# Attention scores in groups of up to three halves, five buffers of exps, single buffers for three other tiles

## The chip, the cores and the metric

The kernel runs on one core of a Trainium2 chip. The metric is the device time of one execution in microseconds. TensorE (PE) does the matmuls, VectorE (DVE), ScalarE (ACT) and GpSimd (POOL) the elementwise work, and SyncE (SP) issues the DMAs of the main part.

## The reference

One adaptive-LayerNorm transformer block in float32, for two batches of 2048 tokens with width 256. Attention has 16 heads with keys of 16 and values of 64; the softmax runs over the *queries* (axis 1 of `bnhm`), so its sum belongs to a key and can be folded into that key's row of values. The feed-forward part quantizes its inputs and weights to FP4 in blocks of 16 and has a hidden width of 704.

```python
mod = (silu(c) @ wmod).reshape(2, 6, 1, 256)
sa, ca, ga, sb, cb, gb = mod[:, 0], ..., mod[:, 5]
# ga and gb are kept at least 0.25 away from zero, with their signs
h = layernorm(x) * (1 + ca) + sa
q, k, v = h @ query_proj, h @ key_proj, h @ value_proj     # 16 heads: 16, 16, 64
sim = einsum('bnkh,bmhk->bnhm', q, k)                      # n query, m key
attn = softmax(sim / 4, axis=1)                            # over the queries
x = x + ga * (einsum('bnhm,bmhv->bnhv', attn, v) @ output_proj)
h = layernorm(x) * (1 + cb) + sb
gate, y = fp4(h) @ fp4(w_gate).T, fp4(h) @ fp4(w_up).T
x = x + gb * (fp4(silu(gate) * y) @ fp4(w_down).T)
```

## The kernel before

**The steps.** Attention is cut into 512 steps: 2 batches x 16 heads x 16 tiles of 128 keys. A step computes 128 x 2048 scores (keys on partitions, queries along the row), in two *halves* of 1024 queries. `scores` (L1009) issues the four matmuls of a step to PSUM: a half is two matmuls of 512 queries, which run as two row tiles of 64 rows (the keys and queries are stacked in a high and a low part). `step` (L1036) then
- evacuates each half with one DVE instruction, which scales, copies it to the exp buffer `e` in SBUF and keeps the minimum of each row,
- joins the two minima on POOL (`mn`),
- takes the exp of all 2048 in place on ACT, with the sum `z`,
- takes the reciprocal `rz` on DVE and scales the key's 64 values by it on POOL (`vn`),
- multiplies on PE: `o` accumulates 64 x 2048 over the 16 steps of a head, as products of `vn` with `e`, in two parts `j` of two column tiles of 64 columns.

So PE has three tilings: two row tiles for scores ("rows"), two column tiles for o, values, projections and most of the other products ("columns"), and the full array, for transposes among others.

**Other work.** Beside the steps run: LayerNorm and q, k projections (`norm`, `qk`, L903, whose results go through `st` to a scratch in DRAM), the values of each group of four heads (`load_wv`, L968, and `values`, L976), the projection of a group of four heads back to x (`load_wo`, L1117, and `project`, L1126), the exact quantization of the weights (beside the first batch's steps), and the feed-forward part of batch 0 (`ffn`, L1240), beside the steps of batch 1. After the last step come the last projection and the feed-forward part of batch 1 (`tail`, L1354).

**What sets the order.** All instructions of PE, DVE, ACT and POOL are emitted by a planner, `Order` (L102), when the program is built. Each piece of work is a generator that yields its next operation or a `Wait` for keys and for *rooms*, which are counted buffers. `rooms` (L367) has 3 places `s` in PSUM for halves of scores, 2 for `o`, 4 for `e`, 2 for heads and so on. The planner keeps a clock for every engine with estimated costs (`estimate`, L269). In `run` (L166) it looks at all chains that can go on, takes for each engine the one with the earliest *due time* among those that could start within a small patience, and emits the operation of the engine that starts first. The engines then work through their queues in that order, with semaphores where data or buffers need them. A room holds the time at which it comes free by the estimates.

The due time of `scores` and `step` is the step's number i; the products with the values get `due(i + LAG)` (L1073), with `LAG = 4.0`. `scores` takes two places and emits the two halves of a step as one list (L223 emits a list without a break), so no other matmul comes between them. A room of `e` is taken by `step` before the first evacuation and given back after the second part of o.

All operations are made by one helper, so that the profile shows line 255 for nearly all of them; tiles' names tell them apart: `ps` scores, `e` exps, `o` products, `vn` scaled values, `v` values, `op` projections, `st` the q, k store.

Of the kernel before, what the change touches and what calls it, by code (L numbers as in the profile page):

```python
# [10 lines left out]
F32 = mybir.dt.float32  # L11
F32R = mybir.dt.float32r
# [8 lines left out]
P = 128  # L21
# [5 lines left out]
CHANGE = 0.1  # L27
PDVE = 0.04
PACT = 0.05
LAG = 4.0  # L30
HALF = 0.22
WPACE = 0.5
NPACE = 0.2
# [28 lines left out]
class Op:  # L62
    def __init__(self, engine, cost, emit, delay=0.0, table=None, mode=None, port=False):
        self.engine, self.cost, self.emit = engine, cost, emit
        self.delay, self.table, self.mode = delay, table, mode
        self.port = port


class Either:
# [32 lines left out]
class Order:  # L102
# [17 lines left out]
    def add(self, gen, due, pace=0.0):  # L120

        heapq.heappush(self.later, (due, next(self.seq), gen, pace))


    def signal(self, key, of=1, early=0.0):

        n, t = self.counts.get(key, (0, 0.0))
        n, t = n + 1, max(t, self.chain.end - early)
        self.counts[key] = (n, t)
        if n == of:  # L130
            self.done[key] = t
        return n == of

    def give(self, name, n=1, place=0):
        for _ in range(n):
            heapq.heappush(self.rooms[name], (self.chain.end, place))

    def due(self, due):
        self.chain.due = due
# [26 lines left out]
    def run(self):  # L166
        while self.later or self.active:
            while self.later and self.later[0][0] <= self.step + self.ahead:
                due, _, gen, pace = heapq.heappop(self.later)
                c = Chain(gen, due, pace)  # L170
                self.active.append(c)
                self.advance(c)
            best, times = {}, {}
            for c in sorted(self.active, key=lambda c: c.due):
                if not self.settle(c):
                    continue
                what = c.what
                free = isinstance(what, Free)
                what = what.op if free else what
                found = []  # L180
                for op in what.ops if isinstance(what, Either) else (what,):
                    ops = op if isinstance(op, list) else [op]
                    e = ops[0].engine
                    start = max(self.clock[e], c.base)
                    if not free and c.engine is not None:
                        start = max(start, c.end + (self.SAME[e] if e == c.engine else self.CROSS))
                    if e == "PE":
                        times[id(ops)] = start
                        if ops[0].mode != self.mode:
                            t = max(start, self.clock[e] + self.DRAIN[self.mode])  # L190
                            times[id(ops)] = t + self.LOAD[ops[0].mode]
                            start = max(start, self.clock[e] + CHANGE)
                    if ops[0].port:
                        start = max(start, self.port)
                    found.append((start, c.due, next(self.seq), c, ops))
                if isinstance(what, Best):
                    ends = [f[0] + sum(op.cost for op in f[4]) for f in found]
                    first = ends[0] - what.margin
                    found = [found[0] if first <= min(ends[1:]) else found[1]]
                for f in found:  # L200
                    best.setdefault(f[4][0].engine, []).append(f)
            if not best:
                if not self.later:
                    raise RuntimeError(
                        "no chain can go on: "
                        + str([(c.due, vars(c.what)) for c in self.active[:20]])
                    )
                self.step = self.later[0][0] - self.ahead
                continue
            picks = []  # L210
            for e, found in best.items():
                first = min(f[0] for f in found)
                start, due, _, c, ops = min(
                    (f for f in found if f[0] <= first + self.patience.get(e, 0.0)),
                    key=lambda f: f[1:3],
                )
                picks.append((start, due, next(self.seq), c, ops))
            start, _, _, c, ops = min(picks)
            e = ops[0].engine
            t = start  # L220
            if e == "PE":
                t = times[id(ops)]
            for op in ops:  # L223
                if op.table is not None and op.table != self.table:
                    t, self.table = t + self.TABLE, op.table
                op.emit()
                t += op.cost
            self.clock[e] = t
            if ops[-1].port:
                self.port = t  # L230
            if e == "PE":
                self.mode = ops[-1].mode
            c.end, c.engine = t + ops[-1].delay, e
            c.due += c.pace
            self.advance(c, e)
# [81 lines left out]
def adaln_block(  # L317
# [41 lines left out]
        for n, e in (  # L359
# [6 lines left out]
    )  # L366
    order = Order(  # L367
        rooms=dict(
            misc=MISC, s=3, o=2, e=4, head=2, osb=1, v=5, x=2, wv=2, wo=2,
            h=2, qm=2, h2=2, h2t=1, hqt=1, st=2, qs=3, ln=2,  # L370
        ),
        ahead=AHEAD,
        patience={"PE": PPE, "DVE": PDVE, "ACT": PACT},
# [7 lines left out]
    ps_s = ctx.enter_context(tc.tile_pool(name="ps_s", bufs=1, space=PSUM))  # L381
    hp = ctx.enter_context(tc.tile_pool(name="hp", bufs=1))
    headp = ctx.enter_context(tc.tile_pool(name="headp", bufs=2))
    spool = ctx.enter_context(tc.tile_pool(name="spool", bufs=4))
    op_ = ctx.enter_context(tc.tile_pool(name="op", bufs=3))
    vp = ctx.enter_context(tc.tile_pool(name="vp", bufs=5))
    w2 = ctx.enter_context(tc.tile_pool(name="w2", bufs=2))
# [2 lines left out]
    def banks(place, name):  # L390

        return ps_s.tile([P, 2, 512], F32, tag=f"s{place}", name=name)
# [13 lines left out]
    def matmuls(dst, pairs, first=True):  # L406
        return [
            T.matmul(dst, lhsT=l, rhs=r, start=(first and k == 0), stop=(k == len(pairs) - 1))
            for k, (l, r) in enumerate(pairs)
        ]  # L410
# [492 lines left out]
    def qk(b, blk, i, n):  # L903
# [20 lines left out]
        if room == "v":  # L924
            st = vp.tile([P, 4, QV], F32, tag="v", name=name).bitcast(F32R)
            st = st.rearrange("p (r u) n -> p r (u n)", r=2)
        else:
            st = w2.tile([P, 2, 512], F32R, tag="st", name=name)
        yield A.copy(st[:, 0, :], ps)
        yield V.tensor_tensor(st[:, 1, :], ps, st[:, 0, :], ALU.subtract)  # L930
        leave(place)
# [35 lines left out]

    def load_wv(b, q):  # L968
        yield Wait(take=["wv"])
        wvs[b, q] = op_.tile([P, KC, QV], F32, tag="wv", name=f"wv{b}_{q}", bufs=2)  # L970
        yield S.dma_start(
            wvs[b, q], wv[:, q * QV : (q + 1) * QV].rearrange("(k p) n -> p k n", p=P)
        )
        signal(("wv", b, q))
# [31 lines left out]

    halves = {}

    def scores(i, b, h, m):  # L1009

        if (b, h) == (0, 0):
            yield Wait(["first q", ("first k", m // 4)])
        else:
            yield Wait([("head", b, h)])
        if i > 0:
            yield Wait([("s", i - 1, 1)])
        order.step = i
        q, k = heads[b, h]
        places = yield Wait(take=["s", "s"], early=HALF)
        ops = []  # L1020
        for u, place in enumerate(places):
            ps = banks(place, f"ps{b}_{h}_{m}_{u}")
            halves[i, u] = ps, place
            for g in range(2):
                rows = slice(64 * g, 64 * (g + 1))
                ops += matmuls(
                    ps[:, g, :],
                    [(k[rows, m * P : (m + 1) * P], q[rows, u * 512 : (u + 1) * 512])],
                )
        yield Free(ops)  # L1030
        for u in range(2):
            signal(("s", i, u), early=0.0 if u else HALF)
        if m == NT - 1:
            give("head")

    def step(i, b, h, m):  # L1036

# [78 lines left out]

    def load_wo(b, q):  # L1117
        yield Wait(["mods"], ["wo"])
        w = wos[b, q] = op_.tile([P, 2, D], F32, tag="wo", name=f"wo{b}_{q}", bufs=2)
        yield S.dma_start(w, wo[q * QV : (q + 1) * QV, :].rearrange("(k p) n -> p k n", p=P))  # L1120
        for j in range(2):
            yield Free(G.tensor_tensor(w[:, j, :], w[:, j, :], mod(b, "ga"), ALU.mult)) if j else \
                G.tensor_tensor(w[:, j, :], w[:, j, :], mod(b, "ga"), ALU.mult)
        signal(("wo", b, q))
# [343 lines left out]
        add(values(0, 0, g), -5 if g == 0 else 4 * g - 3)  # L1468
    steps = [(b, h, m) for b in range(B) for h in range(H) for m in range(NT)]
    for i, (b, h, m) in enumerate(steps):  # L1470
        add(scores(i, b, h, m), i)
        add(step(i, b, h, m), i)
        if m == NT - 1:
            add(take_out(b, h), i - 4)
        if m == 2 and i + NT < len(steps):
            add(load_head(*steps[i + NT - m][0:2]), i)
# [101 lines left out]
```

## Time and profile before

| what | value |
|---|---|
| time, median of 3 runs | 1977.5 us (1976.44 to 2165.38) |
| the profiled execution's own time | 1977.45 us |
| its span, first to last instruction | 1975.7 us |
| granted TensorE clock | 0.997 |
| PE busy | 1920.0 us, 97% |
| DVE busy | 1711.3 us, 87% |
| ACT busy | 1325.7 us, 67% |
| POOL busy | 621.0 us, 31% |

A group of the profile reads: line, engine, operation, output<-inputs by tile name, shapes, xcount, then busy time, the mean duration of one in ns, and the idle time of the engine just before these instructions with what ended most of it. PEld are weight loads, which overlap the matmuls. A float32 matmul is two instructions in the profile, and one of scores is one. In a table of stretches, each row has the stretch, its length, and the busy time of PE, PEld, DVE, ACT and POOL with instruction counts, then the clock and the DMA share. In a timeline, each row has start and busy time, with like instructions that follow each other merged.

### The profile page before, as it was taken

To read this page: it belongs to the slowest core of one execution; us is meant where nothing else is said; L and a number is where in the kernel's file an instruction comes from. 1 tells how busy PE (TensorE), PEld (TensorE's weight loads), DVE (VectorE), ACT (ScalarE), POOL (GpSimd) and SP (SyncE) were. 2 spreads that over 40 slices of the span, in tenths; PEclk is the share of its full clock that TensorE was granted. 3 is DMA by queue.
4 is the path that set the end of the run, shared out by engine and by line. 5 is a ranking of instruction groups with operands and counts; after the bars stand their busy time and mean duration, and the time that the engine had idled before them with its cause. 6 is when DMAs were issued, how large, how long until landed. Compare 5 with 4: busy or idle time off the path is not lost. (4 is left out here: it accounts for less than half of the span.)

```text
span 1975.7 us, 30282 instructions
## 1 busy us (share of the span) xinstructions
PE 1920.0 (97%) x10212; PEld 783.1 (40%) x10212; DVE 1711.3 (87%) x4118; ACT 1325.7 (67%) x1419; POOL 621.0 (31%) x1387
## 2 busy tenths in 40 slices
PE   8999999999999989999999999999999999999998
PEld 5323333233333333334333433434443343335666
DVE  5899889989999998778888688898788878997997
ACT  3577766776777676776777667677576867785333
POOL 0233333333344331112445435454343211230010
PEclk9999999999999999999999999999999999999999
DMA  6322121112111122310111201210111111100000
GB/s 213 81 56 58 47 60 49 38 33 49 33 45 33 38 54 75 102 38 25 36 48 46 65 25 46 54 36 16 26 35 43 33 33 33 33 1 1 11 14 19
DMA packets 40394, 88.01 MB, mean 45 GB/s; under 512 B 6320, under 2 KB 22576, under 8 KB 36272
## 3 DMA queue, kind: packets, MB, share of 16 engines
q1 hardware_dynamic: 38880, 83.98, 16.4%
q10 hardware_dynamic: 1360, 2.10, 0.3%
q8 instruction: 82, 1.34, 0.3%
q14 instruction: 72, 0.59, 0.1%
HBM read 63.51 MB, written 20.97 MB: 43 GB/s over the span
## 5 line engine op out<-in xcount | busy, mean ns | idle before, releaser
L255 DVE TENSOR_SCALAR_CACHE_REDUCE e<-ps 128x1024 f32<-128x1024 f32 x1024 | 1221.9, 1218 | 142.1 <-PE ps L255 93.2
L255 ACT ACTIVATE e<-e,mn 128x2048 f32<-128x2048 f32 x512 | 1025.3, 2003 | 436.6 <-POOL mn L255 433.3
L255 PE MATMUL o<-e,vn 128*64 128x512 f32 x4096 | 996.7, 604 | 24.1 <-POOL vn L255 18.5
L255 PEld LDWEIGHTS o<-e,vn 128*64 128x64 f32 x4096 | 253.7, 136 | 482.7 <-issue 351.7
L255 POOL TENSOR_SCALAR mn<-mn 128x1 f32<-128x1 f32 x512 | 154.2, 301 | 834.1 <-DVE rz L255 344.4
L255 PE MATMUL ps<-q,k 64*128 64x512 f32 x2048 | 383.8, 449 | 5.4 <-DVE e L255 2.0
L255 PEld LDWEIGHTS ps<-q,k 64*128 64x128 f32 x2048 | 157.5, 185 | 377.8 <-DVE rz L255 109.5
L255 POOL TENSOR_SCALAR vn<-v,rz 128x64 f32<-128x64 f32 x512 | 169.4, 331 | 307.1 <-DVE rz L255 235.7
L255 PE MATMUL op<-wo,osb 128*64 128x256 f32 (+1 forms) x960 | 125.3, 382 | 2.5 <-DVE x L255 1.8
L255 PE MATMUL v<-wv,ht 128*64 128x256 f32 x1024 | 124.2, 385 | 0.6 <-DVE st L255 0.6
L255 DVE RECIPROCAL rz<-z 128x1 f32<-128x1 f32 x512 | 80.4, 157 | 27.0 <-ACT e L255 25.8
L255 PEld LDWEIGHTS op<-wo,osb 128*64 128x64 f32 (+1 forms) x960 | 76.2, 140 | 60.7 <-issue 30.7
L255 ACT ACTIVATION_READ_ACCUMULATOR e<-e,mn 128x1 f32 x512 | 95.4, 186 | 0.0
L255 PEld LDWEIGHTS v<-wv,ht 128*64 128x64 f32 x1024 | 70.9, 138 | 59.0 <-issue 26.8
L255 DVE DVE_READ_ACCUMULATOR e<-ps 128x1 f32 x1024 | 84.9, 83 | 0.0
L255 ACT COPY osb<-o 64x512 f32<-64x512 f32 x101 | 58.4, 579 | 18.6 <-PE o L255 17.2
L255 PE MATMUL qk<-ht,wqk_sb 128*64 128x512 f32 (+1 forms) x224 | 65.8, 605 | 1.3 <-ACT ht L255 0.9
L255 POOL TENSOR_TENSOR h<-h,m 128x704 f32<-128x704 f32 x32 | 54.1, 1691 | 10.7 <-DVE m L255 6.1
L255 DVE TENSOR_TENSOR x<-op,x 128x1024 f32<-128x1024 f32 (+2 forms) x33 | 37.0, 1122 | 17.8 <-PE op L255 17.6
L255 PE MATMUL dn<-wdb,e 117*128 117x256 f32 (+1 forms) x192 | 45.1, 383 | 3.7 <-ACT e L255 3.7
L255 ACT ACT_TABLE_LOAD x34 | 43.6, 1283 | 4.5 <-issue 3.9
L255 PE MATMUL dn<-wd_t,h2t 117*64 117x256 f32 (+1 forms) x384 | 46.2, 383 | 0.2 <-DVE h2t L255 0.2
(243 smaller groups left out, 1452.4 us busy)
## 6 DMA issues: line engine op xcount, KB each, us to landing
k<-scr SPq DMA_DIRECT2D x124, 256.0 KB, 4.7
scr<-st SPq DMA_DIRECT2D x32, 512.0 KB, 3.1
q<-scr SPq DMA_DIRECT2D x124, 128.0 KB, 5.6
x<-in_x_dram SPq DMA_DIRECT2D x8, 512.0 KB, 4.5
wv<-in_wv_dram SPq DMA_DIRECT2D x8, 256.0 KB, 5.3
wo<-in_wo_dram SPq DMA_DIRECT2D x8, 256.0 KB, 4.1
xt<-in_x_dram SPq DMA_DIRECT2D x4, 512.0 KB, 5.9
out_dram<-h2t SPq DMA_DIRECT2D x16, 128.0 KB, 1.7
```

What stands on the lines that cost most here:

```text
L255: op = Op(self.name, *self.estimate(method, args, kw, lambda: f(*args, **kw)))
```

## The change

`scores` is now one generator for a head instead of one for a step. It takes two places (or one, where only one half is left), as before, and makes a `Group` of the halves. Before the planner emits a group, it asks it to grow: a third half is added if less than three are in it, if a place `s` is free, if that place's time is no later than the estimated time at which the third half would start, and, where the half is the first of a step, if an exp buffer is free by then too. The next group begins where this one ended, so after a group of three the groups straddle two steps, until another group of three or the end of the head.

Beside this, there are five exp buffers instead of four, LAG is 4.5 instead of 4.0, and the tiles `wv` (value weights), `wo` (projection weights) and `st` (q, k store) have one buffer instead of two.

```diff
-LAG = 4.0
+GROUP = 3
+LAG = 4.5
...
+class Group(list):
+    grow = staticmethod(lambda t: False)
...
             if e == "PE":
                 t = times[id(ops)]
+            while isinstance(ops, Group) and ops.grow(t):
+                pass
             for op in ops:
...
-            misc=MISC, s=3, o=2, e=4, head=2, osb=1, v=5, x=2, wv=2, wo=2,
-            h=2, qm=2, h2=2, h2t=1, hqt=1, st=2, qs=3, ln=2,
+            misc=MISC, s=3, o=2, e=5, head=2, osb=1, v=5, x=2, wv=1, wo=1,
+            h=2, qm=2, h2=2, h2t=1, hqt=1, st=1, qs=3, ln=2,
...
-    spool = ctx.enter_context(tc.tile_pool(name="spool", bufs=4))
+    spool = ctx.enter_context(tc.tile_pool(name="spool", bufs=5))
...
-            st = w2.tile([P, 2, 512], F32R, tag="st", name=name)
+            st = w2.tile([P, 2, 512], F32R, tag="st", name=name, bufs=1)
...
-        wvs[b, q] = op_.tile([P, KC, QV], F32, tag="wv", name=f"wv{b}_{q}", bufs=2)
+        wvs[b, q] = op_.tile([P, KC, QV], F32, tag="wv", name=f"wv{b}_{q}", bufs=1)
...
-    def scores(i, b, h, m):
...
+    def scores(i, b, h):
+        n = 0
+        while n < 2 * NT:
+            m = n // 2
...
+            if i + n > 0:
+                yield Wait([("s", i + (n - 1) // 2, (n - 1) % 2)])
+            due(i + n / 2)
+            places = yield Wait(take=["s"] * min(2, 2 * NT - n), early=HALF)
+            group = Group()
...
+            def grow(t):
+                t += sum(op.cost for op in group) - order.CROSS
+                m = n // 2
+                if len(group) == 2 * GROUP or n == 2 * NT or not order.rooms["s"]:
+                    return False
+                if (b, h) == (0, 0) and ("first k", m // 4) not in order.done:
+                    return False
+                if n % 2 == 0 and not (order.rooms["e"] and order.rooms["e"][0][0] <= t):
+                    return False
+                if order.rooms["s"][0][0] > t:
+                    return False
+                half(heapq.heappop(order.rooms["s"])[1])
+                return True
+
+            for place in places:
+                half(place)
+            group.grow = grow
+            first = n - len(places)
+            yield Free(group)
+            order.step = i + (n - 1) // 2
+            for j in range(first, n):
+                signal(("s", i + j // 2, j % 2), early=HALF * (n - 1 - j))
+        give("head")
...
-        w = wos[b, q] = op_.tile([P, 2, D], F32, tag="wo", name=f"wo{b}_{q}", bufs=2)
+        w = wos[b, q] = op_.tile([P, 2, D], F32, tag="wo", name=f"wo{b}_{q}", bufs=1)
...
-        add(scores(i, b, h, m), i)
+        if m == 0:
+            add(scores(i, b, h), i)
```

More of the change, by code (lines that the diff above doesn't have):

```diff
@@ L1007, in adaln_block, with half @@
     halves = {}
-    def scores(i, b, h, m):
[L1011 to L1034, printed above, removed]
+    def scores(i, b, h):
+        n = 0
+        while n < 2 * NT:
+            m = n // 2
+            if (b, h) == (0, 0):
+                yield Wait(["first q", ("first k", m // 4)])
+            elif n == 0:
+                yield Wait([("head", b, h)])
+            if i + n > 0:
[3 more added lines that the diff above has]
+            group = Group()
+            q, k = heads[b, h]
+            def half(place):
+                nonlocal n
+                m, u = n // 2, n % 2
+                n += 1
+                ps = banks(place, f"ps{b}_{h}_{m}_{u}")
+                halves[i + m, u] = ps, place
+                for g in range(2):
+                    rows = slice(64 * g, 64 * (g + 1))
+                    group.extend(
+                        matmuls(
+                            ps[:, g, :],
+                            [(k[rows, m * P : (m + 1) * P], q[rows, u * 512 : (u + 1) * 512])],
+                        )
+                    )
+            def grow(t):
[20 more added lines that the diff above has]
+        give("head")
```

## The prediction

> **What bounds the kernel now.** I read the busy times first, then the costliest groups, then the stretches, then TensorE's own timeline.
>
> ```profile
> PE 1920.0 (97%) x10212; PEld 783.1 (40%) x10212; DVE 1711.3 (87%) x4118; ACT 1325.7 (67%) x1419; POOL 621.0 (31%) x1387
> ...
> L255 DVE TENSOR_SCALAR_CACHE_REDUCE e<-ps 128x1024 f32<-128x1024 f32 x1024 | 1221.9, 1218 | 142.1 <-PE ps L255 93.2
> L255 PE MATMUL o<-e,vn 128*64 128x512 f32 x4096 | 996.7, 604 | 24.1 <-POOL vn L255 18.5
> L255 PE MATMUL ps<-q,k 64*128 64x512 f32 x2048 | 383.8, 449 | 5.4 <-DVE e L255 2.0
> ```
>
> TensorE (PE) is busy 97% of the 1975.7 us span, so it bounds the kernel, with VectorE (DVE) next at 87%. The idle time ahead of the two big groups of matmuls is 24.1 and 5.4 us. Whatever can be won has to be won in PE's own time or in its few waits. The stretches say where those are (columns: length, then busy us of PE, PEld, DVE, ACT, POOL).
>
> ```profile
> 100.00:700.00 600.00, 584.05 (x3076) 208.71 (x3072) 553.58 (x1308) 434.45 (x446) 211.92 (x515) 1.00 0.18 44
> 700.00:1600.00 900.00, 886.27 (x4990) 344.71 (x4990) 755.36 (x1765) 633.17 (x664) 333.80 (x673) 1.00 0.17 44
> 1600.00:1800.00 200.00, 195.21 (x996) 66.71 (x992) 173.56 (x352) 149.61 (x149) 46.15 (x145) 1.00 0.11 25
> ```
>
> From 100 to 1800 us PE is idle for 1700 - 584.05 - 886.27 - 195.21 = 34.5 us. In the first of these stretches DVE is 92% busy (553.58 of 600): there it has little slack. After that it has 16%.
>
> A busy PE isn't a PE at its peak, so I looked at the starts in its timeline (start, then busy us).
>
> ```profile
> 1245.30 0.73 PE L255 MATMUL ps<-q,k 64*128 64x512 f32 x4
> 1245.97 2.80 PE L255 MATMUL o<-e,vn 128*64 128x512 f32 x12
> 1248.69 0.73 PE L255 MATMUL ps<-q,k 64*128 64x512 f32 x4
> 1249.35 2.80 PE L255 MATMUL o<-e,vn 128*64 128x512 f32 x12
> 1252.08 0.73 PE L255 MATMUL ps<-q,k 64*128 64x512 f32 x4
> 1252.74 1.94 PE L255 MATMUL o<-e,vn 128*64 128x512 f32 x8
> ```
>
> PE alternates between two tilings: scores (64*128, two row tiles) and exps times values (128*64, two column tiles). Each visit to the scores is four matmuls, that is two halves. Start to start it takes 0.66 to 0.67 us. Visits of o straight before a visit of scores have medians of 1.009, 1.867 and 2.726 us for 4, 8 and 12 instructions over the whole trace: 0.858 us for each four, and 0.15 us that doesn't grow with the work. That constant part, and its like in the visits to the scores, is what the change is about.
>
> **What the Trainium skill says.** TensorEngine Tiling (Array Packing), section Tiling Modes, says that changing the tiling mode drains TensorE. The trace agrees: those 0.15 us, and the larger sum of 0.24 us worked out below for a visit to the scores. PSUM — Partial Sum Buffer, section Engine vs sequencer instructions, says that the queues of ScalarE, VectorE and GpSimd are strict FIFO, and that matmuls start and complete in program order. The trace agrees as far as it goes: DVE waited 93.2 us for scores, although other work of its own stood behind. So a score whose place isn't free holds all matmuls behind it, and an evacuation without a buffer holds DVE.
>
> **The change part by part.** How often PE changes tiling follows from the two programs' instruction order.
>
> 1. *Third half.* Before, there are 512 visits to the scores, all of two halves. After, 502: 458 of two, 32 of three, 12 of one (an odd last half of a head). Other neighbours shift as well. Changes of tiling, before to after: scores to columns 485 to 483, columns to scores 492 to 473, full array to columns 49 to 39, columns to full 42 to 49, full to scores 20 to 29, scores to full 27 to 19. In all 1115 to 1092.
>    The price of one: single matmuls of a visit to the scores at 606.28 us start at 606.278, 606.617 and (next visit) 606.943. The first matmul is shown as 498 ns and the third as 394, so 0.104 us of the first gap is the entry, and a half alone takes at most 0.337 - 0.104 = 0.233 us. A 512-column matmul of o follows its like after 0.429 us; I take half of its stream for a half of scores, 0.2133 us, an estimate that lies under the bound. So a visit to the scores has 0.663 - 2 x 0.2133 = 0.236 us over its work, and the other kinds 0.153 to 0.166 us.
>    Sum: -2 x 0.236, -19 x 0.160, -10 x 0.157, +7 x 0.157, +9 x 0.154, -8 x 0.237 = -4.5 us; the work itself is the same. Bounds: if a half costs 0.233 us, 10 visits to the scores save 0.36 each instead of 0.39, and the sum is -4.2. If the whole 0.33 us were a half's own (nothing shared in a visit), only the drain of 0.16 goes with each pair of changes: about -2. I take -4.4, as nearly all of it is on PE's path and PE has no slack.
> 2. *Five exp buffers, LAG 4.5.* The products with the values come later: in the order of PE, with these durations added up, the mean distance from a step's last score to its first product grows from 9.1 to 10.7 us. The chain between is an evacuation (1.22 + 0.08 us), POOL's minimum (0.30), the exp (2.00 + 0.19), the reciprocal (0.16) and POOL's scaled values (0.33): 4.3 us, and handoffs. Steps with under 6.2 us fall from 41 to 22. Those under 5.8 us rise from 4 to 18. PE waited 18.5 us, 34 times, for the scaled values. By shares of the 41 tight steps, 19 fewer are worth 18.5 x 19/41 = -8.6 us; the 14 very tight ones, at the mean wait of 18.5/34 = 0.54 us, cost +7.6. I take -1, with bounds of -17 (half of all idle time) and +14 (each very tight step at 1.0 more than I say, less a part that overlaps).
> 3. *Third half against its place.* The nearest distance of a third half from the end of the half three before it is 2.53 us. In the kernel before, 137 second halves stand at 2.53 and 32 at 1.67. Two evacuations take 2.6. So the third half asks for no more than second halves did: nothing, and if that cover is gone, a part of an evacuation (up to 1.3 us) on 32 visits.
> 4. *One buffer for wv, wo and st.* On SP's queue the loads of wv and wo move back behind the release of their only buffer, and heads' loads are queued behind them. The closest is the second wv. Its buffer is free at 78 us of PE's work, and behind it are the loads of the second head, first used at 97. Four issues take about 2.5 us, the landings 4.7 and 5.6: some 12 of 19 us. Everywhere else at least 40 us lie between. The st store lands 3.1 us after its issue, and the copy and subtraction into st take 0.58 and 0.69. The closest row of eight such chains has 22 steps of 3.9 us for them, 10.7 each. I cost all three at nothing: the scores' own progress hides them. Without that cover it is one load of about 10 us, once.
> 5. *Work moved between engines.* DVE takes 6 more copies of 118x768 (953 ns) and gives up 5 of osb (687 ns) and seven smaller ones, about 0.3 to 0.5 us each: near 0. They lie in the second batch's part, where DVE has its 16%. In the tail the order of a few rows changes, POOL gives one product of 128x704 to DVE (0.8 us), and the distance of the evacuations from their use stays: 0, within 3 either way.
>
> Sum: -4.4 - 1 = -5.4 us. The profiled execution took 1977.45 us for a span of 1975.7, and the median shown is 1977.5, so 1977.5 - 5.4 = **1972 us**.
>
> **Rivals.**
> - *Waits melt.* The fifth buffer lets the products lag so far that PE no longer waits. For it: beyond 8.2 us of distance PE hardly waited in the trace of before, and such steps grow from 245 to 337. Against it: only 34.5 us of idle time is there, and much of it is not on this chain. Half of it and the 4.4: 1956 us.
> - *DVE held by the exp buffers (slower).* After a third half the pairs straddle two steps. A step's first half is then issued ahead of the product that frees its exp buffer (five steps back): in 40 of 507 steps, where before it was none. The evacuation stands in DVE's FIFO, and what is queued behind (reciprocals, other scores) is held, and the PE waits for places. Added up on PE's order, the holds are 1.3 to 5.6 us each, 71 in all, if DVE is always there early. The 20 or so steps in the first batch are the ones that can hurt, as DVE is 92% busy there. Half of 35 us for these, less the 4.4: 1990 us; in full, 2008. It decides from about 0.3 us a held step on (4.4 + 1 over 20). Against it: DVE is rarely ahead where it is 92% busy, so it is seldom early enough to be held.
> - *The change does little of what it says.* 32 visits out of 512 are threes. Random shifts of waits as large as the gain: 1977 us. I count this in the forecast's own case.
>
> **Numbers.** Forecast's case (1963 to 1979 us): 0.64. Waits melt (1948 to 1963): 0.12. DVE held, or tight steps dearer than I say (1979 to 2020): 0.24. The range of 8 in 10 is 1958 to 1990. About 2% (40 us) is what a measurement of this kernel can tell from no change: faster by more than that needs all the idle time and more, 0.01; slower by more, the last rival in full and some mishap, 0.03.
>
> **What would show it.** Right: PE's visits to the scores with six matmuls take 0.88 us start to start, and there are 32; PE's busy time falls by about 4 us; the wait of o for vn stays between 10 and 25 us. Wrong in part 1: 0.99 us for such a visit. The rival of DVE: evacuations that wait for PE's o in steps 60 to 71, 125 to 143 and 422 to 449. Part 4: PE waiting for a DMA of k, q or wv. What would make it wrong altogether: DVE's or ACT's order having turned against PE in a way that the distances on PE alone don't show.

## The result, and the profile after

The changed kernel takes 1956.4 us (median of 4 runs, 1956.12 to 1957.12), against 1977.0 before: a ratio of 0.9897, 95% interval 0.9878 to 0.9917. That is 20.6 us less. One of the four executions before took 2165.4 us; without it the median before is 1976.4 and the gain 20.1 us. The forecast was 1972 with a range of 1958 to 1990. So the sign and the first part of the sum were right and the size was not: the time lies where the rival "waits melt" had it (1956).

The same lines of the page as before: busy times, and the three groups.

```profile
PE 1910.6 (98%) x10212; PEld 782.6 (40%) x10212; DVE 1704.3 (87%) x4114; ACT 1327.6 (68%) x1427; POOL 619.8 (32%) x1387
...
L264 DVE TENSOR_SCALAR_CACHE_REDUCE e<-ps 128x1024 f32<-128x1024 f32 x1024 | 1225.4, 1216 | 123.9 <-PE ps L264 96.1
L264 PE MATMUL o<-e,vn 128*64 128x512 f32 x4096 | 991.8, 603 | 14.6 <-POOL vn L264 10.4
L264 PE MATMUL ps<-q,k 64*128 64x512 f32 x2048 | 379.7, 447 | 5.5 <-DVE e L264 2.0
```

PE does the same 10212 instructions in 9.3 us less busy time, and the idle time ahead of the products `o` falls from 24.1 to 14.6 us. DVE is busy for 7.0 us less and ACT for 1.9 us more.

The stretches, with the columns of before:

```profile
100.00:700.00 600.00, 589.22 (x3116) 210.84 (x3114) 564.18 (x1341) 440.85 (x452) 215.21 (x522) 1.00 0.19 46
700.00:1600.00 900.00, 891.24 (x5052) 348.69 (x5048) 755.90 (x1765) 640.00 (x676) 333.78 (x678) 1.00 0.18 45
```

PE idles 19.5 us in these 1500 us; before it was 29.7. The stretch from 100 to 700 us now holds 40 more of its matmuls.

PE's timeline shows a group of three halves (six matmuls) and one of two (four):

```profile
469.43 1.46 PE L264 MATMUL o<-e,vn 128*64 128x512 f32 x6
470.81 1.09 PE L264 MATMUL ps<-q,k 64*128 64x512 f32 x6
471.84 3.65 PE L264 MATMUL o<-e,vn 128*64 128x512 f32 x16
475.42 0.73 PE L264 MATMUL ps<-q,k 64*128 64x512 f32 x4
```

This visit of three takes 1.03 us start to start, more than most. The median of the 32 is 0.897, that of the twos 0.663 and that of the ones 0.431. The three medians differ by 0.232 and 0.234, so a half costs 0.233 us, and a visit 0.198 us once.

**Where the 22 us of the span went.** I split the starts of PE's matmuls, from the first score to the last (the *steps*), into three terms: the work (0.2325 us a half; 0.858 us each two 512-column products side by side, and in proportion), the changes of tiling (0.198 us a visit to the scores, 0.153 for any other stretch in one tiling), and what is left, the *late starts*. The work comes to 1496.4 us before and 1496.5 us after, so that with the table each sums up to its span.

| us | before | after |
|---|---|---|
| until the first score | 44.6 | 43.4 |
| changes of tiling in the steps | 193.5 | 189.3 |
| late starts in the steps | 56.9 | 38.3 |
| after the last score | 184.3 | 186.2 |

So the changes of tiling give 4.2 us and the late starts 18.6. Of these 18.6 us, 13.7 were idle time of PE in the steps (36.6 us before, 22.9 after); the rest stood in its busy time. Of the late starts (counting those over 0.06 us), those of `o` went from 33.0 to 22.8, those of scores from 8.7 to 6.6, and those of all other work from 16.1 to 9.7. So 8.4 of the 18.6 us are not on the chain from a step's scores to its products, and no experiment below takes them apart. Part of this is the clock: after a wait of PE at 613 us the trace of before shows 3.4 us at half clock, which is up to 1.7 us of late starts. It isn't there in the trace of after. After the first 100 us, the traces of 8 of the 20 kernels here have such a stretch in the steps (one has two), each of 3.4 us, so the late starts of two traces can differ by some 2 us for this alone.

### The profile page after: what moved, and what is told of

It reads as the page before. It is cut to its first block, busy times and chain, and to the rows that moved or that the text cites. A ratio compares the mean times of both kernels' runs of the same rounds, so it can differ in the third digit from the quotient of the medians.

```text
span 1953.7 us, 30223 instructions
## 1 busy us (share of the span) xinstructions
PE 1910.6 (98%) x10212; PEld 782.6 (40%) x10212; DVE 1704.3 (87%) x4114; ACT 1327.6 (68%) x1427; POOL 619.8 (32%) x1387
## 5 line engine op out<-in xcount | busy, mean ns | idle before, releaser
L264 PE MATMUL o<-e,vn 128*64 128x512 f32 x4096 | 991.8, 603 | 14.6 <-POOL vn L264 10.4
L264 PE MATMUL ps<-q,k 64*128 64x512 f32 x2048 | 379.7, 447 | 5.5 <-DVE e L264 2.0
```

What stands on the lines that cost most here:

```text
L264: op = Op(self.name, *self.estimate(method, args, kw, lambda: f(*args, **kw)))
```

## The experiments

The question was which part makes the late starts fall: the distance from scores to products (LAG and the fifth buffer), the groups of three, the rewritten generator of scores, or the luck of one order out of many. *Distance* means below what it does in the prediction: the mean time on PE's order from the end of a step's last score to its first product, worked out from the order and the durations of work and tiling changes. The names in the text and the tables (`lag_alone` and so on) are those of the runs.

### One part at a time

All of the change but the groups:

```diff
-LAG = 4.0
+LAG = 4.5
-  s=3, o=2, e=4, ... wv=2, wo=2, ... st=2
+  s=3, o=2, e=5, ... wv=1, wo=1, ... st=1      # and the pools' bufs likewise
```

> The kernel before with five exp buffers, single wv, wo and st, and LAG 4.5: all of the change but the groups of three. If the extra distance between scores and products melts the waits, this has most of the gain: 1957 to 1963 us. If the groups of three make it (fewer tiling changes, and what else they shift), 1972 to 1978. If neither alone does, about 1968.

Measured: 1967.0 us (1965.5 to 1967.5), ratio 0.9951 (0.9936 to 0.9965). Late starts are 44.7 us, those of `o` 27.1, changes of tiling 193.0. The third expectation fits (about 1968, neither part alone): it is about half of the gain.

The groups alone, in the changed kernel:

```diff
-LAG = 4.5
+LAG = 4.0
-  e=5, wv=1, wo=1, st=1
+  e=4, wv=2, wo=2, st=2
```

> The changed kernel with four exp buffers, LAG 4.0 and two buffers of wv, wo and st: the groups of up to three halves alone. With four buffers only 17 threes form and the tiling changes rise to 1118 (1115 before). If the distance makes the gain: 1974 to 1982 us. If the groups make it: 1957 to 1965.

Measured: 1971.8 us, ratio 0.9977 (0.9968 to 0.9986). It lies between the two expectations: 5 us of gain. Late starts of `o` stay at 33.1.

LAG alone, in the kernel before (`LAG = 4.0` to `4.5`):

> The kernel before with LAG 4.5 and nothing else, so with four exp buffers. The distance can hardly grow with four buffers (mean 9.4 us on PE's order, 9.1 before, 10.7 after). If distance makes the gain: 1972 to 1978 us. If LAG works by due times alone, without the buffer: below 1965.

Measured: 1970.0 us, ratio 0.9965 (0.9952 to 0.9978). Late starts are 50.5 us. That is 2 us below the first range: 7 us of gain, with a distance of 9.4 us against 9.1. A little better than the distance would have it.

The buffers alone, in the kernel before (as the first edit, LAG left at 4.0):

> The kernel before with five exp buffers and single wv, wo and st, LAG 4.0. With LAG 4.0 the planner's order is the same as with four buffers and single wv, wo and st, so the fifth buffer can only loosen waits on the chip. If the distance makes the gain: 1974 to 1979 us. If the chip's own waits for a free exp buffer were the cause: below 1968.

Measured: 1976.3 us, ratio 1.0002 (0.9993 to 1.0011): nothing, as expected, with a distance of 9.2 us. At LAG 4.0, in the kernel before, the fifth buffer is worth nothing.

### Is it luck?

Two constants that the change leaves as they are were moved, each in both kernels, to get other orders: the planner's patience on DVE, and its allowance for the place of a later half (which both generators of scores use).

```diff
-PDVE = 0.04
+PDVE = 0.05          # first pair
-HALF = 0.22
+HALF = 0.24          # second pair
```

> The kernel before with the planner's patience on DVE at 0.05 instead of 0.04, a constant that has nothing to do with the change; the order turns out different all over. PE's order has 1110 tiling changes and a mean distance of 9.04 us from scores to products. If the change works by distance and tiling changes: 1972 to 1980 us. If orders differ by luck as much as the gain: anywhere from 1956 to 1998.

> The changed kernel with the same patience on DVE, 0.05. 1098 tiling changes, mean distance 10.64 us. If the change works by distance and tiling changes: 1955 to 1961 us. If luck: anywhere from 1940 to 1985.

> The kernel before with the planner's allowance for the second half's place (HALF) at 0.24 instead of 0.22. 1113 tiling changes, mean distance 9.11 us. Distance and tiling changes: 1973 to 1980 us. Luck: 1956 to 1998.

> The changed kernel with HALF at 0.24. Only 20 groups of three form here, 1105 tiling changes (13 more than the change), mean distance 10.99 us. Distance makes most of the gain, and the groups their tiling changes: 1957 to 1963 us. If the threes themselves make the waits fall: 1962 to 1969. Luck: 1940 to 1985.

Measured: 1978.6 and 1962.9, then 1976.6 and 1960.1 us. The second lies 2 us above the range for distance and tiling changes, the others within theirs. Within a pair the change gives 15.7 and 16.5 us, and 20.1 to 20.6 in the original. So an order varies by some 2 us in the kernel before and by up to 6.5 in the changed one. The change's own order looks like a good draw from many: about 16 us in both other pairs, so that some 4 may be the draw. Two pairs are few, and a difference of less than some 6 us between two changed kernels shows nothing by itself. The second shuffled kernel after has only 20 threes and still has low late starts (40.3 us), which speaks for distance and against the threes.

### The chain between scores and products

The order of all engines is kept; only the chain is shortened. The values are scaled by a constant column, so the product no longer waits for the reciprocal of the exps' sum. The softmax's division is left out, so the output is another one:

```diff
         yield G.tensor_scalar(
             vn,
             vs[b, h // 4, m // 4][:, m % 4, (h % 4) * VD : (h % 4 + 1) * VD],
-            rz,
+            magic[:, 0:1],
```

> The kernel before, with the same order on every engine, but the values are scaled by a constant column instead of the reciprocal of the exps' sum, so the softmax's division is left out. Scores, exps and products all run. The chain from the last score to the product loses the reciprocal and the scaling (0.16 + 0.33 us and two handoffs). If PE's waits ahead of o (33 us in the trace of before, counted as starts later than work and tiling changes explain) come from this chain being longer than the distance: 1960 to 1968 us. If PE waits for something else there (places, the exp buffers, weights): 1974 to 1979.

> The changed kernel with the same constant column, the division left out. With the longer distance fewer steps are short of it, so there is less to win: 1946 to 1953 us if the chain is what remains of the waits ahead of o (23 us), 1954 to 1958 if what remains has other causes.

Measured: 1971.9 us, ratio 0.9982 (0.9975 to 0.9989), and 1953.7 us. The groups of `o` and `ps` in the kernel before with the short chain:

```profile
L255 PE MATMUL o<-e,vn 128*64 128x512 f32 x4096 | 994.9, 603 | 18.0 <-POOL vn L255 12.5 <-DVE osb L255 2.7 <-ACT osb L255 1.7
L255 PE MATMUL ps<-q,k 64*128 64x512 f32 x2048 | 385.1, 449 | 7.4 <-DVE e L255 4.1 <-DMA q<-st 1.9 <-DVE rz L255 0.9
```

Idle time ahead of `o` falls from 24.1 to 18.0 us, and late starts of `o` from 33.0 to 26.2 (from 22.8 to 16.2 in the changed kernel). That the end of this chain holds PE is shown, since nothing else was changed. The trace of before agrees: of 62 first products that start late, 51 start within 0.2 us of the end of their scaled values. But the kernel before wins 4 to 5 us, not 9 to 17, and lies between the two expectations; some of it comes back as waits ahead of `ps` (5.4 to 7.4). The changed kernel wins 2.7 us, and its time lies between the two expectations. The scaled values are ready 0.63 us sooner in the mean (6.42 instead of 7.05 us after a step's last score, in the kernel before), and that takes 6.8 of the 33.0 us; the rest of the chain was not shortened.

### Undoing one part

The changed kernel with groups of at most two (`GROUP = 2`), and with `LAG = 4.0`:

> The changed kernel with groups of two halves at most: five exp buffers, LAG 4.5 and the new generator of scores, no threes. 1108 tiling changes, mean distance 11.0 us. If the threes bring what is missing between distance alone (1967 us) and the change (1956): 1964 to 1970. If it is the new generator's other timing of the steps: 1955 to 1960.

> The changed kernel with LAG back at 4.0: groups of three (30 of them, 1094 tiling changes), five exp buffers, mean distance 9.5 us instead of 10.7. If distance makes three fifths of the gain: 1964 to 1970 us. If the threes with a fifth buffer make it: 1956 to 1961.

Measured: 1961.8 us, ratio 0.9931 (0.9916 to 0.9946), and 1967.2 us (1965.5 to 1970.7), 0.9957 (0.9941 to 0.9974). Without threes 5.4 us are lost, between the two expectations: 3.2 of changes of tiling (192.5 against 189.3) and 2.7 of late starts. That is no more than another order can do. Without LAG 10.8 us are lost, as the first expectation has it and more than the 6.5 us of another order, and nearly all of it in late starts (51.0 us, those of `o` 34.9, as before). The group of `o` in that kernel:

```profile
L264 PE MATMUL o<-e,vn 128*64 128x512 f32 x4096 | 990.3, 603 | 25.3 <-POOL vn L264 21.5 <-DVE osb L264 1.7 <-ACT osb L264 1.2
```

With LAG at 4.0 the idle time ahead of `o` is back at 25.3 us, groups of three or not.

The changed kernel with four exp buffers, and with more LAG:

```diff
-  s=3, o=2, e=5,
+  s=3, o=2, e=4,       # four_buffers
-LAG = 4.5
+LAG = 5.0              # lag_5
```

> The changed kernel with four exp buffers: LAG 4.5 and groups of three stay. The distance falls to 9.4 us and only 13 threes form (1110 tiling changes). If the buffer is what lets the distance grow: 1965 to 1971 us, with over 48 us of waits in the steps (38 in the change). If LAG does it alone: 1955 to 1961.

> The changed kernel with LAG 5.0. Five buffers bound the distance: 10.9 us, hardly more than with 4.5, 1106 tiling changes and 28 steps under 6.2 us. If distance is what counts: 1957 to 1962 us, the 14 more tiling changes being the difference. If a later due time brings more by itself: below 1955.

Measured: 1971.5 us, ratio 0.9974 (0.9967 to 0.9982), and 1968.6 us, 0.9966 (0.9953 to 0.9979). The first lies half a us above the range for the buffer as what lets the distance grow; its distance is 9.4 us and its late starts of `o` are 31.2. The second is 12 us slower than the change and a clear miss: its distance is 10.9 us, yet its late starts are 46.4. Some of the waits of DVE in it (total us, times, longest):

```profile
DVE e L264 <- PE ps L264: 85.1, 149, 2.2
DVE rz L264 <- ACT e L264: 37.9, 42, 2.6
DVE x L264 <- PE op L264: 16.0, 15, 5.8
DVE e L264 <- PE o L264: 13.0, 12, 2.6
```

The last line is an evacuation that waits for an exp buffer which a product still reads. That is the slower rival of the prediction. In the orders of this table it is there wherever LAG asks for more than the buffers have:

| kernel | exp buffers, LAG | evacuations waiting for `o`, us |
|---|---|---|
| before | 4, 4.0 | none |
| lag_alone | 4, 4.5 | 21.1 |
| four_buffers | 4, 4.5 | 29.9 |
| buffers_alone, pairs_only, lag_undone | 5, 4.0 or 4.5 | none |
| the change | 5, 4.5 | 0.8 |
| lag_5 | 5, 5.0 | 13.0 |

With four buffers and LAG 4.0 the new generator already has 13.3 us (groups_alone) and 15.2 (generator_alone). So the fifth buffer is what lets LAG 4.5 and the groups be used without holding DVE. It is worth nothing at LAG 4.0, 3 us in the kernel before with LAG 4.5 (`lag_alone` against `lag_and_buffers`), and 15 us in the changed kernel.

That the held evacuations are what costs this time is not shown. All evacuations together wait less in each of the five kernels with over 10 us of them than in the kernel before, where it was 142.1 us. First `lag_alone`, then `four_buffers`:

```profile
L255 DVE TENSOR_SCALAR_CACHE_REDUCE e<-ps 128x1024 f32<-128x1024 f32 x1024 | 1222.2, 1217 | 111.7 <-PE ps L255 51.2
L264 DVE TENSOR_SCALAR_CACHE_REDUCE e<-ps 128x1024 f32<-128x1024 f32 x1024 | 1221.4, 1216 | 115.0 <-PE ps L264 66.1
```

And `lag_alone`, with 21.1 us of them, is 7 us faster than the kernel before, which has none. The shorter distance of four buffers gives some 9 of the 15 us by the line further below (7.0 us for each us of distance); the rest, and why `lag_5` is slow, stay open.

### The generator

```diff
-GROUP = 3               # generator_alone, with LAG 4.0, e=4, wv=2, wo=2, st=2
+GROUP = 2
...
             due(i + n / 2)
+            order.step = i + n // 2         # step_early
...
             yield Free(group)
-            order.step = i + (n - 1) // 2   # step_early
```

> The changed kernel with groups of two at most, four exp buffers, LAG 4.0 and two buffers of wv, wo and st: only the generator is rewritten. 1122 tiling changes (7 more than before), mean distance 9.2 us. If the rewritten generator is a part of the gain by itself: 1970 to 1974 us. If it isn't: 1976 to 1980.

> The changed kernel with the planner's step moved forward before a group takes its places, as the kernel before does, instead of after it is emitted. 30 groups of three, 1096 tiling changes, mean distance 10.7 us. If the later step is what the new generator gives: 1960 to 1965 us. If not: 1955 to 1959.

Measured: 1974.7 us, ratio 0.9990 (0.9981 to 0.9998), between the two expectations, and 1960.1 us, at the lower edge of the first, for a later step that matters. But 4 us are within what another order does to the changed kernel, so this decides nothing. The rewritten generator by itself is worth some 2 us. Why `pairs_only` is 5 us faster than `lag_and_buffers`, which has the same buffers, LAG and group size, isn't settled: the draw of the order (up to 6.5 us) is enough for it, but that isn't shown.

### What the account forecasts

> The changed kernel with LAG 4.25. 36 groups of three and only 2 of one: 1077 tiling changes, 15 fewer than with 4.5, and a mean distance of 10.4 us. If tiling changes cost 0.18 us each and the distance is nearly kept: 1951 to 1956 us. If LAG 4.5 matters as such: 1957 to 1963.

> The changed kernel with the planner's patience on PE at 0.14 instead of 0.12. 23 groups of three, 1095 tiling changes, mean distance 11.2 us, and 9 steps under 6.2 us instead of 22. If short steps make what is left of the waits ahead of o: 1951 to 1956 us. If they don't: 1956 to 1962.

The edits are `LAG = 4.25`, and `PPE = 0.14`, the planner's patience on PE. Measured: 1961.0 us, ratio 0.9921 (0.9906 to 0.9936), a miss for the count of tiling changes and inside the range for LAG 4.5 as such: the changes of tiling fell by 2.8 us as counted, but late starts rose by 7.5 (with a distance of 10.4 us). And 1956.8 us, 0.9900 (0.9885 to 0.9915), in the range for short steps that don't matter, and as fast as the change: with 9 steps under 6.2 us of distance instead of 22 the late starts of `o` are 2.5 us less, and 1.0 comes back in changes of tiling. None of these beats the change, and both differences are within what another order does.

### All orders together

| kernel | us | changes of tiling | all late starts | late starts of `o` | distance |
|---|---|---|---|---|---|
| the change | 1956.4 | 189.3 | 38.3 | 22.8 | 10.7 |
| patience_014 | 1956.8 | 190.3 | 38.7 | 20.3 | 11.2 |
| shuffled_after_2 | 1960.1 | 191.8 | 40.3 | 20.5 | 11.0 |
| step_early | 1960.1 | 190.2 | 41.7 | 27.5 | 10.7 |
| lag_425 | 1961.0 | 186.5 | 45.8 | 24.0 | 10.4 |
| pairs_only | 1961.8 | 192.5 | 41.0 | 21.6 | 11.0 |
| shuffled_after_1 | 1962.9 | 190.3 | 42.9 | 27.3 | 10.6 |
| lag_and_buffers | 1967.0 | 193.0 | 44.7 | 27.1 | 10.9 |
| lag_undone | 1967.2 | 189.7 | 51.0 | 34.9 | 9.5 |
| lag_5 | 1968.6 | 192.1 | 46.4 | 27.9 | 10.9 |
| lag_alone | 1970.0 | 192.5 | 50.5 | 28.2 | 9.4 |
| four_buffers | 1971.5 | 192.5 | 52.9 | 31.2 | 9.4 |
| groups_alone | 1971.8 | 193.1 | 52.8 | 33.1 | 9.0 |
| generator_alone | 1974.7 | 194.3 | 54.6 | 29.9 | 9.2 |
| buffers_alone | 1976.3 | 193.8 | 53.7 | 34.9 | 9.2 |
| shuffled_before_2 | 1976.6 | 193.3 | 57.6 | 35.6 | 9.1 |
| before | 1977.0 | 193.5 | 56.9 | 33.0 | 9.1 |
| shuffled_before_1 | 1978.6 | 192.7 | 54.0 | 31.7 | 9.0 |

Over these 18 orders the late starts go with the mean distance: a straight line falls by 7.0 us for each us of distance (correlation -0.94), and single orders lie up to 4.7 us off it. From 9.07 to 10.73 us the line gives 11.7 of the 18.6 us. The number of steps under 5.8 us of distance has no relation to them (-0.06). The orders form two clusters, at 9.0 to 9.5 us and at 10.4 to 11.2, and most of the line is the step between them. A line through different orders isn't proof; the short chain, which keeps the order, and LAG undone are what tie the late starts of `o` to it.

## Why the prediction was wrong

**The bound.** Right: the gain is all on PE's line. PE's busy time fell by 9.3 us where the sign was about 4, because late time is in it too; the wait of `o` for `vn` is 10.4 us, just inside the 10 to 25 that was named.

**Third half (part 1).** Right in its sum: -4.4 was taken, and the counted stretches with the measured medians give 4.2. The size of a half was at the upper bound given, 0.233 us, not the 0.2133 of the estimate; so a visit of three takes 0.90 us, and the 0.88 that I named as the sign is a little short. Without groups of three the changed kernel takes 5.4 us more (`pairs_only`), 3.2 of them by this term; the other 2 can be the draw of an order.

**Five exp buffers, LAG 4.5 (part 2): the step that failed.** "I take -1, with bounds of -17 and +14": measured, the late starts fell by 18.6 us, those of `o` by 10.2. Three terms of its sum were mis-sized.
- The stock of waits was too small. I used the 18.5 us that the profile puts down to POOL's scaled values ahead of PE's own `o`. Counted from the starts, `o` was late by 33.0 us, and all matmuls of the steps by 56.9: late time that the page shows as busy is in it too. For the same reason the 34.5 us of idle time was not all there was to win.
- The very tight steps were priced at 0.54 us each above what others cost, +7.6 in all. Counted from the starts, the 18 steps under 5.8 us waited 5.4 us together after, and the 4 of before 2.9: +2.5.
- The steps over 6.2 us were left out. The chain was put at 4.3 us and handoffs; in the trace of before, the scaled values were ready 7.05 us after a step's last score in the mean (6.90 after the change). So steps with more than 6.2 us waited too: first products of steps with 6.2 to 8.2 us of distance were late by 14.1 us in all before and 9.7 after, those under 6.2 us by 12.7 and 6.4.

These terms are about `o`. For the other 8.4 us, late starts of scores and other work, the prediction has no term, and their cause stays open. About 4 of the 20.6 us may be the draw of this order, which no term of mine could have given, though a range that allows for it would have.

**Places (part 3) and single buffers (part 4).** Right. PE's wait for a score's place is 2.0 us as before, no DMA of `wv`, `wo` or `st` holds PE, and `buffers_alone` takes the time of before.

**Moved work (part 5).** Right: the time after the last score is 1.9 us more, within the 3 given.

**Rivals.** "Waits melt", at 0.12, was right on the time, and in part on the mechanism: the waits shrank, but `o` is still late by 22.8 of 33.0 us. That its sum meets the time to within 1 us is in part luck: it took half of the idle time without saying why half, and the draw of the order may be in the result. The argument against it (only 34.5 us of idle time) was the error named above. "DVE held" is absent in the change, 0.8 us in one wait: the 40 steps found on PE's order aren't reached early by DVE. But such waits are real, and one buffer fewer or half a step of LAG more brings them out (30 and 13 us) in kernels that lose most of the gain. That they cause the loss is not shown.

## What to carry to other kernels

A planner's lag and its buffer count are one setting. Here the fifth buffer alone was worth nothing, LAG 4.5 alone 7 us, and the two together 10, in the kernel before; more lag than the buffers have brought held evacuations on the engine that fills them. Take the stock of waits from the starts of the bounding engine's instructions, less work and switches, rather than from its idle time: here 36.6 us of idle time in the steps stood against 56.9 us of late starts. And before a gain of 1% in a planned order is put down to a part of the change, move a constant that the change leaves alone in both kernels: here that was worth up to 6.5 us by itself.

## What the runs showed of the hardware

- A visit to the scores costs 0.198 us once and 0.233 us a half, from visits of one, two and three halves (0.431, 0.663, 0.897 us). With visits of two alone the two terms couldn't be told apart.
- In the kernel before, the wait of PE at 612.8 to 614.9 us (gaps of 0.27, 0.73 and 0.34 us) is followed by 3.4 us at half clock from 615.5 us, in which a visit to the scores took 1.15 us and one of four `o` instructions 1.72, against 0.66 and 1.01:

```profile
612.83 0.51 PE L255 MATMUL ps<-q,k 64*128 64x512 f32 x2 [0.27 <-DVE e L255]
614.07 0.50 PE L255 MATMUL ps<-q,k 64*128 64x512 f32 x2 [0.73 <-DVE e L255]
614.91 1.44 PE L255 MATMUL o<-e,vn 128*64 128x512 f32 x4 [0.34 <-POOL vn L255]
616.28 1.22 PE L255 MATMUL ps<-q,k 64*128 64x512 f32 x4
617.43 1.80 PE L255 MATMUL o<-e,vn 128*64 128x512 f32 x4
619.15 0.73 PE L255 MATMUL ps<-q,k 64*128 64x512 f32 x4
```

  That the waits cause it is not shown: the waits of 1.18 us at 737.0 and of 1.06 us at 744.8 in the same trace had no such stretch behind them.
